# Selective scan: the last-column copies of the scans kept in PSUM, moved from ScalarE to VectorE

## The chip, the cores and the metric

The kernel runs on one core of a Trainium2 chip. Times are microseconds (us) of the device; the figure compared is the median of several executions. The engines are called PE (TensorE; its weight loads are PEld), DVE (VectorE), ACT (ScalarE), POOL (GpSimd) and SP (SyncE, which here only issues DMAs). Each works through a list of its own in order, and an instruction waits at the head of its list until what it needs is done.

## The reference

The program is four network layers on a tensor of 8 images, 64 channels, 64 x 64 pixels. The change is in the fourth, whose core is a recurrence over the 4096 pixels of an image, in four directions `k`, for 128 channels with 16 states each:

```python
def step(h, inp):
    u_t, dt_t, B_t, C_t = inp
    h = h * jnp.exp(dt_t[..., None] * A) + dt_t[..., None] * B_t[:, :, None, :] * u_t[..., None]
    return (h, jnp.einsum('bkcn,bkn->bkc', h, C_t))
```

So a state `h` decays by `exp(dt*A)`, takes in `dt*B*u`, and is read out through `C`, summed over the 16 states.

## The kernel before

**Pairs and stages.** The images are worked in four pairs. `tile_kernel` (L1909) starts with the front of pair 0 (layers 0 to 2 and the sources of layer 3). Then `scans(p)` (L1659) runs the recurrence of pair p, and between its steps it draws pieces of other work from a generator: the back of pair p-1 and the front of pair p+1. While the front is in its attention, `self.dense` is 1. In the last pair there is only back work beside the scans.

**Units and steps.** The 4096 pixels are cut into 8 chunks of `TD` = 512 columns. A unit is one image, one direction and one chunk, 64 units for a pair. `at` counts the chunks of a direction: a chunk starts from the last column of the chunk before, which is kept in `self.carries` (one column per scan of a unit, 16), and the last chunk (`at == NTD - 1`) leaves none. A unit has 8 steps of two states each, and a step has two scans (`j` = 0 and 1), one for each half of the channels: 64 channels by 2 states fill the 128 partitions.

**One step** (`step`, L1756):

- ACT computes `exp(dt*A)` into a PSUM bank `dad` (L1776). The banks come from a ring of three (tag `da`); once the back work of the last pair runs out of its planned share, from that ring and another of three in turn.
- DVE runs the scan over the 512 columns (L1779). Its result goes to SBUF (`hd`), or in place into the PSUM bank (`dad`). How many of the two scans stay in PSUM is `own`: 0 or 1 in turn, and 1, 1, 1, 2 in dense stretches and for the last pair.
- If a next chunk follows, ACT copies the last column of the result to `carries` (L1787).
- The product with C (L1790, L1793) is made by POOL for scans in SBUF and by DVE for scans in PSUM, into `vd`.

Two steps ahead, POOL makes `vd = B * (dt*u)` (L1754, `products`); two or three steps behind, PE sums the products over states (L1805, `sums`). SP fetches rows of B and C for each step into rings of four tiles (L1746, `fetch`), so a fetch waits until the tile four steps back was read. Once per unit `inputs` (L1711) and `spread` (L1731) prepare `dt` and `dt*u` of the next unit: PE matmuls, ACT, one DVE product (L1735), and two DMAs that spread it over partitions (`du`, L1739), issued by SP behind the fetches.

**What orders the work.** Each engine's list is not in the order of the program text. The framework plans it when the program is built, by modelled times; only pairs given to `behind` (L444) are pinned. It also sets all waits. In the trace, DVE's product of a scan in PSUM usually stands one scan later than in the text, behind the first scan of the next step.

Of the kernel before, what the change touches and what calls it, by code (L numbers as in the profile page):

```python
# [24 lines left out]
TD = 512  # L25
NTD = L // TD
# [1133 lines left out]
class _Direct:  # L1160
# [595 lines left out]
    def step(self, i, st):  # L1756

        nc, w, net = self.nc, self.w, self.net
        wk, ps = self.sw, self.ps
        u = self.units[i // 8]  # L1760
        k, c, at, CC, v = u["k"], u["c"], u["at"], st["C"], st["v"]


        n0 = 2 * (i % 8)
        own = 1 + (i % 4 == 3) if u["image"] >= B - 2 or self.dense else i % 2
        rev = k >= 2

        def along(t):
            return t[:, ::-1] if rev else t

        h = wk.tile([P, 2 - i % 2, TD], F32, name="hd", tag=f"h{i % 2}", bufs=2)
        hs = []
        for j in range(2):
            n = n0 + j
            da = self.bank("dad", (P, TD), "da")
            nc.scalar.activation(da, u["du"][:, j, 0], AF.Exp, scale=net.As[:, k, n : n + 1])  # L1776
            first = 0.0 if at == 0 else self.carries[:, n : n + 1]
            to = da if j >= 2 - own else h[:, j]
            nc.vector.tensor_tensor_scan(along(to), along(da), along(v[:, j]), first, ALU.mult, ALU.add)  # L1779
            hs.append(to)  # L1780
            if at < NTD - 1 and (own or j):
                ends = h[:, :, 0] if rev else h[:, :, TD - 1]
                cs = self.carries[:, n0 : n0 + 2]
                if own:
                    ends = to[:, 0:1] if rev else to[:, TD - 1 : TD]
                    cs = self.carries[:, n : n + 1]
                nc.scalar.activation(cs, ends, AF.Copy)  # L1787

        if own == 0:
            st["w"] = nc.gpsimd.tensor_tensor(v, h, self.twice(CC), ALU.mult)  # L1790
        for j in range(2 if own else 0):
            engine = nc.vector if j >= 2 - own else nc.gpsimd
            m = engine.tensor_tensor(v[:, j], hs[j], CC, ALU.mult)  # L1793
            st.setdefault("w", m)

    def sums(self, i, st, after=None):

        nc, w, net = self.nc, self.w, self.net
        wk, ps = self.sw, self.ps
        u = self.units[i // 8]  # L1800
        k, c = u["k"], u["c"]
        if i % 8 == 0:
            u["y"] = ps.tile([P, TD], F32, name="yd", tag="y", bufs=1)
        for j in range(2):
            m = nc.tensor.matmul(  # L1805
                u["y"][self.HALF[j]], lhsT=w["fold"], rhs=st["v"][:, j], start=(i % 8 == 0), stop=(i % 8 == 7)
            )
            if after is not None and j == 0:
                net.behind(m, after)
# [147 lines left out]
```

## Time and profile before

| what | value |
|---|---|
| median of 3 runs (lowest to highest) | 12742.49 us (12727.7 to 12745.85) |
| profiled execution, its own time | 12767.64 us |
| span of that execution | 12765.8 us |
| busy share PE, DVE, POOL, ACT | 77%, 68%, 59%, 55% |
| scans in PSUM, DVE product each (L1793) | 1824 |
| last-column copies by ACT from PSUM (L1787, `carry<-dad`) | 1594, 168 ns each |
| last-column copies by ACT from SBUF (L1787, `carry<-hd`) | 1559, 200 ns each on average |

The busy share of an engine is an average over stages with different limits. The scans begin at about 1848 us; before that the front of pair 0 runs alone. From then on three times an attention stretch (1867 to 2802, 5006 to 5848, 7977 to 8804 us) is followed by the rest of that front and a back (to 10450 us), and the last pair's scans end at about 12650 us. In the waits, "X <- Y: 232.0, 154, 7.7" says that X found its engine idle 232.0 us in all, in 154 cases, 7.7 us at most, until Y was done. In a timeline a bracket gives the idle time before the instruction and what ended it.

### The profile page before, as it was taken

To read this page: it belongs to the slowest core of one execution; us is meant where nothing else is said; L and a number is where in the kernel's file an instruction comes from. 1 tells how busy PE (TensorE), PEld (TensorE's weight loads), DVE (VectorE), ACT (ScalarE), POOL (GpSimd) and SP (SyncE) were. 2 spreads that over 40 slices of the span, in tenths; PEclk is the share of its full clock that TensorE was granted. 3 is DMA by queue.
4 is the path that set the end of the run, shared out by engine and by line. 5 is a ranking of instruction groups with operands and counts; after the bars stand their busy time and mean duration, and the time that the engine had idled before them with its cause. 6 is when DMAs were issued, how large, how long until landed. Compare 5 with 4: busy or idle time off the path is not lost. (4 is left out here: it accounts for less than half of the span.)

```text
span 12765.8 us, 142485 instructions
## 1 busy us (share of the span) xinstructions
PE 9843.7 (77%) x46358; PEld 3333.1 (26%) x46358; DVE 8687.9 (68%) x10259; ACT 7009.2 (55%) x15693; POOL 7550.7 (59%) x3844
## 2 busy tenths in 40 slices
PE   9888879987887667997888756997888855555556
PEld 2255222223342112222443211222433211111111
DVE  0122256777786776668776679467777679998878
ACT  5533247765663655665665555665566365455444
POOL 0000026677776683667776676467777567777874
PEclk9966779997888778998888877998888967777667
DMA  0000024544443462444443454344444356556554
GB/s 19 1 1 1 6 98 145 150 146 133 133 128 111 145 189 81 138 140 145 125 131 113 128 176 144 93 140 142 126 134 129 100 174 183 170 165 186 171 172 123
DMA packets 779703, 1575.84 MB, mean 123 GB/s; under 512 B 89280, under 2 KB 89408, under 8 KB 778176
## 3 DMA queue, kind: packets, MB, share of 16 engines
q1 hardware_dynamic: 754752, 1510.30, 39.4%
q10 hardware_dynamic: 24192, 56.32, 1.2%
q8 instruction: 367, 6.01, 0.2%
q14 instruction: 392, 3.21, 0.1%
HBM read 1197.16 MB, written 100.66 MB: 102 GB/s over the span
## 5 line engine op out<-in xcount | busy, mean ns | idle before, releaser
L1754 POOL TENSOR_TENSOR vd<-B,du 128x1024 f32<-128x1024 f32 x2048 | 4821.4, 2371 | 3295.1 <-DMA B<-rows 2016.1
L1805 PE MATMUL yd<-vd,pack 128*64 128x512 f32 x8192 | 2946.2, 738 | 933.7 <-POOL vd L1793 595.3
L1776 ACT ACTIVATE dad<-du,As 128x512 f32<-128x512 f32 x4096 | 2733.8, 682 | 1122.5 <-DVE vd L1793 458.5
L1779 DVE TENSOR_TENSOR_SCAN hd<-dad,carry,vd 128x512 f32<-128x512 f32 x1992 | 2497.0, 1267 | 480.0 <-ACT dad L1776 324.4
L1793 POOL TENSOR_TENSOR vd<-hd,C 128x512 f32<-128x512 f32 x1290 | 1659.8, 1290 | 1046.7 <-DVE hd L1779 1030.0
L1779 DVE TENSOR_TENSOR_SCAN dad<-dad,carry,vd 128x512 f32<-128x512 f32 x1592 | 2004.8, 1273 | 166.6 <-ACT dad L1776 164.4
L1790 POOL TENSOR_TENSOR vd<-hd,C 128x1024 f32<-128x1024 f32 x491 | 1158.1, 2359 | 735.5 <-DVE hd L1779 406.6
L1307 ACT ACTIVATE e<-s 128x512 f32<-128x512 f32 x2048 | 1200.2, 591 | 628.3 <-PE s L1301 626.5
L1301 PE MATMUL s<-X 64*128 64x512 f32 x4096 | 1435.8, 646 | 79.6 <-ACT e L1307 58.8
L1805 PEld LDWEIGHTS yd<-vd,pack 128*64 128x64 f32 x8192 | 667.0, 160 | 2815.0 <-issue 1214.6
L1793 DVE TENSOR_TENSOR vd<-dad,C 128x512 f32<-128x512 f32 x1824 | 1207.5, 673 | 239.6 <-ACT carry L1787 232.0
L1293 PE MATMUL po<-e,VT 128*64 128x512 f32 x4096 | 1207.8, 623 | 16.9 <-ACT e L1307 10.2
L1459 PEld LDWEIGHTS w_av<-vals,wide 64*64 64x64 f32 x16384 | 678.1, 173 | 209.7 <-ACT wide L1449 106.3
L1459 PE MATMUL w_av<-vals,wide 64*64 64x9 f32 x16384 | 705.6, 224 | 34.8 <-ACT wide L1449 34.6
L1787 ACT ACTIVATE carry<-hd 128x1 f32<-128x1 f32 (+1 forms) x1559 | 307.6, 200 | 697.1 <-DVE hd L1779 681.0
L1301 PEld LDWEIGHTS s<-X 64*128 64x128 f32 x4096 | 393.4, 186 | 1107.5 <-issue 832.6
L1787 ACT ACTIVATE carry<-dad 128x1 f32<-128x1 f32 x1594 | 268.1, 168 | 698.3 <-DVE dad L1779 688.9
L1717 PE MATMUL pdd<-xs,xdt 128*128 128x512 f32 x512 | 375.7, 824 | 334.6 <-issue 103.1
L1444 DVE TENSOR_TENSOR wide<-w_s,bias 128x512 f32<-128x512 f32 x512 | 327.7, 680 | 254.5 <-PE w_s L1431 246.5
L1449 ACT ACTIVATE wide<-wide 128x512 f32<-128x512 f32 x512 | 309.5, 626 | 318.7 <-DVE wide L1444 194.3
L1239 PE MATMUL pv<-n_sq,pack 128*128 128x512 f32 x576 | 364.5, 718 | 144.0 <-ACT n_sq L1237 130.0
L1316 DVE COPY att<-po 128x512 f32<-128x512 f32 x32 | 21.7, 679 | 643.3 <-PE po L1293 643.3
(246 smaller groups left out, 11137.5 us busy)
## 6 DMA issues: line engine op xcount, KB each, us to landing
B<-rows SPq DMA_DIRECT2D x2048, 256.0 KB, 3.6
C<-rows SPq DMA_DIRECT2D x2048, 256.0 KB, 3.5
du<-du SPq DMA_DIRECT2D x512, 512.0 KB, 5.9
xs<-xt SPq DMA_DIRECT2D x128, 256.0 KB, 3.6
xs<-xc SPq DMA_DIRECT2D x128, 256.0 KB, 3.8
xc<-xcv ACTq DMA_DIRECT2D x64, 256.0 KB, 2.1
zs<-z ACTq DMA_DIRECT2D x64, 256.0 KB, 3.8
xt<-XT ACTq DMA_DIRECT2D x32, 512.0 KB, 4.6
```

The source lines that it names most:

```text
L1293: nc.tensor.matmul(po[half[im]], lhsT=VT[:, t, half[im]], rhs=es[im], start=(t == 0), stop=(t == 31))
L1301: nc.tensor.matmul(ss[im], lhsT=at(half[im], t), rhs=X[half[im], jc * CH : (jc + 1) * CH], start=True, stop=True)
L1307: nc.scalar.activation(e, ss[im], AF.Exp, scale=C**-0.5, accum_out=parts[:, im, t, jc : jc + 1])
L1459: nc.tensor.matmul(self.av[half[im], x % 4 + j, h, :], lhsT=es[h // 4][half[im], j, h % 4, :], rhs=V[half[im], x + j, h, :], start=True, s ...
L1717: nc.tensor.matmul(pd, lhsT=net.xdt[:, k, :], rhs=x, start=True, stop=True)
L1754: self.nc.gpsimd.tensor_tensor(v, self.twice(st["B"]), self.units[i // 8]["du"][:, :, 1], ALU.mult)
L1776: nc.scalar.activation(da, u["du"][:, j, 0], AF.Exp, scale=net.As[:, k, n : n + 1])
L1779: nc.vector.tensor_tensor_scan(along(to), along(da), along(v[:, j]), first, ALU.mult, ALU.add)
L1787: nc.scalar.activation(cs, ends, AF.Copy)
L1790: st["w"] = nc.gpsimd.tensor_tensor(v, h, self.twice(CC), ALU.mult)
L1793: m = engine.tensor_tensor(v[:, j], hs[j], CC, ALU.mult)
L1805: m = nc.tensor.matmul(u["y"][self.HALF[j]], lhsT=w["fold"], rhs=st["v"][:, j], start=(i % 8 == 0), stop=(i % 8 == 7))
```

## The change

For scans that stay in PSUM the copy of the last column is taken from ACT and given to DVE, in the program text right behind the DVE product with C. Scans in SBUF keep their copy on ACT: with `own == 0` one copy of two columns after the second scan, else one copy behind the scan that went to SBUF. The condition on the ACT copy changes accordingly.

```diff
@@ -1778,7 +1778,7 @@
             to = da if j >= 2 - own else h[:, j]
             nc.vector.tensor_tensor_scan(along(to), along(da), along(v[:, j]), first, ALU.mult, ALU.add)
             hs.append(to)
-            if at < NTD - 1 and (own or j):
+            if at < NTD - 1 and (j if own == 0 else to is not da):
                 ends = h[:, :, 0] if rev else h[:, :, TD - 1]
                 cs = self.carries[:, n0 : n0 + 2]
                 if own:
@@ -1792,6 +1792,9 @@
             engine = nc.vector if j >= 2 - own else nc.gpsimd
             m = engine.tensor_tensor(v[:, j], hs[j], CC, ALU.mult)
             st.setdefault("w", m)
+            if at < NTD - 1 and j >= 2 - own:
+                end = hs[j][:, 0:1] if rev else hs[j][:, TD - 1 : TD]
+                nc.vector.tensor_copy(self.carries[:, n0 + j : n0 + j + 1], end)
```

## The prediction

> **What bounds the kernel now.** I read the page's first part, then busy time by stretches, because the shares of the whole hide the stages.
>
> ```profile
> span 12765.8 us, 142485 instructions
> PE 9843.7 (77%) x46358; PEld 3333.1 (26%) x46358; DVE 8687.9 (68%) x10259; ACT 7009.2 (55%) x15693; POOL 7550.7 (59%) x3844
> ```
>
> No engine is full. In the stretches the columns are length, then PE, PEld, DVE, ACT and POOL busy:
>
> ```profile
> 1867.00:2802.00 935.00, 900.22 (x2995) 243.49 (x2994) 662.85 (x701) 653.50 (x1877) 653.10 (x350) 0.98 0.50 148
> 2802.00:5006.00 2204.00, 1625.94 (x8918) 607.24 (x8916) 1691.64 (x2011) 1216.12 (x2316) 1559.30 (x759) 0.79 0.45 138
> ...
> 10450.00:11650.00 1200.00, 674.95 (x1450) 149.21 (x1450) 1084.73 (x1156) 623.17 (x1348) 936.87 (x497) 0.73 0.58 175
> 11650.00:12450.00 800.00, 419.81 (x889) 93.06 (x890) 648.52 (x687) 357.09 (x857) 640.01 (x347) 0.69 0.56 174
> ```
>
> So there are four regimes. A, attention (three times, 2604 us): PE 96% busy. B, the rest of fronts and backs (three times, 5979 us): nobody over 80%, DVE and PE lead, each list held up by the others. C1 (1200 us): DVE 90%. C2 (800 us): 81% DVE, 80% POOL, and a pattern that repeats every 32.5 us. C3, the last 200 us of scans: DVE 93%.
>
> Next, the copies and the waits around them, over the whole trace:
>
> ```profile
> L1787 ACT ACTIVATE carry<-dad 128x1 f32<-128x1 f32 x1594 | 268.1, 168 | 698.3 <-DVE dad L1779 688.9 <-issue 5.9
> ```
>
> ```profile
> ACT carry L1787 <- DVE dad L1779: 688.9, 1091, 4.5
> ACT dad L1776 <- DVE vd L1793: 458.5, 508, 9.5
> DVE vd L1793 <- ACT carry L1787: 232.0, 154, 7.7
> ```
>
> The reader is to see two waits that the change touches: ACT stands in front of the copies until the scan is done, and DVE's product stands until ACT has made the copy, though the two only read the same bank. Asked by regime, the 232 us are 8 in A, 51 in B, 38 in C1, 133 in C2.
>
> [...] The trace has small DVE instructions from PSUM at its start, and I go by these:
>
> ```profile
> 14.43 0.16 DVE L363 TENSOR_TENSOR bq<-pbq,pack 128x1 f32<-128x1 f32 x1 [1.45 <-PE pbq L362]
> 14.50 0.15 DVE L365 TENSOR_TENSOR bk<-pbq,pack 128x1 f32<-128x1 f32 x1
> 14.57 0.14 DVE L366 TENSOR_TENSOR bv<-pbq,pack 64x1 f32<-64x1 f32 x1
> ```
>
> They last 0.15 us but follow each other at 0.07: the tail of one lies over the next. Price of a copy in a busy list: 0.07 us. Ends: 0.04 (the closest spacing of small memsets, at 11026.86 and 11026.90) and 0.15 (no overlap). Below nothing it can't be.
>
> **The change, part by part.**
>
> *A.* 538 copies move. On DVE, 58 to 71% busy here, 538 x 0.07 = 38 us vanish in idle time; if PE were not full they would count. PE itself waited 21 us for ACT copies (16.4 at L1301, 4.6 at L1293, its rows in the three stretches); 538 of the 865 copies here are from PSUM, so 13 us belong to them, of which I credit half, since PE's next wait is often close: -7.
>
> *B.* 492 copies cost 34 us of DVE; 51 us of DVE's waits go. What DVE gains or loses here I count with its busy share, 0.77: (34 - 51) x 0.77 = -13. ACT: I followed its timeline behind each copy from PSUM. Of 248 us waited there, 197 are followed by an idle gap at least as long before the list runs on, because the next instruction waits for the same DVE, or for PE; they only change their name. 51 us are not swallowed. ACT is 55% busy, so I credit a quarter: -13. B: about -26, less 1 for the bank below: -25.
>
> *C1.* 299 copies x 0.07 = 21, on DVE at 90%: +19. The waits, 38 us in 17 cases of up to 5.8: with three banks DVE can use at most a product, a scan and a product (0.59 + 1.18 + 0.59 = 2.36, by the distances in the timeline) before it needs the next exponential from the same held-up ACT. Each wait cut at 2.36, they sum to 25. Net -6.
>
> *C2.* Here the largest part of the wait sits, 5.5 us in each of 24 units, and I credit nothing. One period:
>
> ```profile
> 12057.32 3.71 POOL L1793 TENSOR_TENSOR vd<-hd,C 128x512 f32<-128x512 f32 x3
> ...
> 12058.61 0.51 SPq L1746 DMA_DIRECT2D C<-rows  x1
> ...
> 12059.88 1.20 SPq L1739 DMA_DIRECT2D du<-du  x2
> ...
> 12065.03 1.30 ACT L1776 ACTIVATE dad<-du,As 128x512 f32<-128x512 f32 x2 [7.12 <-DMA du<-du]
> 12066.27 0.15 ACT L1787 ACTIVATE carry<-dad 128x1 f32<-128x1 f32 x1
> ...
> 12066.45 0.69 DVE L1793 TENSOR_TENSOR vd<-dad,C 128x512 f32<-128x512 f32 x1 [5.82 <-ACT carry L1787]
> ...
> 12067.44 4.65 POOL L1754 TENSOR_TENSOR vd<-B,du 128x1024 f32<-128x1024 f32 x2 [6.40 <-DMA du<-du]
> ```
>
> ACT's list has the next unit's exponentials ahead of the old unit's copy, and they wait for `du`. DVE's product waits behind both. But what sets the 32.5 us is a ring without DVE: POOL works from the arrival of `du` without a break (23.4 us) until its product frees a C tile at 12058.57, SP issues that fetch, another, then `du` (1.3), `du` takes 7.5 to reach POOL. After the change DVE finishes the old unit while `du` travels, and is then idle for the next. 213 copies (15 us) fit into that idle time too. Zero. *C3*: 49 copies at 93%: +3.
>
> **Release of banks.** An exponential that reuses a bank now waits for the copy behind the product, 0.07 us later, where it waited for product and ACT copy. Behind it on ACT stand other exponentials and the front's activations, and PE waits for those. In the timelines such an exponential (0.68) is done some 0.4 us before its scan, so this costs about 1 us; at most 508 waits x 0.07 = 36. The later scan that reads `carries` comes 8 steps on and waits for nothing.
>
> **Sum.** -7 - 25 - 6 + 0 + 3 = -35 us against the profiled execution's 12767.6 us (span and 1.8 us around it), 12733. That execution is 0.2% above the median of the runs; scaled by 12742.5 / 12767.6, 12708 us.
>
> **Rivals.**
>
> 1. *The waits only change their name* (no change, about 12740). For it: four fifths of ACT's waits in B are swallowed by the next gap, and C2's ring. Then copies and gains cancel: 12733 to 12750.
>
> 2. *The copies lengthen DVE's list where it leads* (slower). Place: B and C, 1053 copies. Price 0.07 us each, 74 us: 12816; at 0.15, 158 us: 12900. It decides when what is recovered from B and C1 falls below the copies' price, that is when DVE, freed from ACT's copy, mostly meets an exponential that isn't ready. For it: C1 and C3 at 90% and more, and that DVE has most of the busy time in B together with PE. Against: 89 us of DVE's own waits in B and C1 go.
>
> 3. *C2 opens as well* (faster). If the new plan of the lists frees the C tile a product earlier on POOL (2.36 us in 24 units, 57 us), or if `du` is asked for earlier: 12708 - 57, and with the cut in C1 removed about 12630. Against it: POOL has no idle time in that ring but for `du`.
>
> That the change doesn't do what it says, a plan that puts the copy ahead of the product, would cost the same 0.07 us.
>
> **How the numbers follow.** A measurement of this kernel can tell about 0.2%, 25 us, from no change: 12717 to 12768. Chances: my sum 0.38 (faster by over 0.2% in 0.30 of it, within in 0.08), rival 1 0.20 (within 0.16, slower 0.04), rival 2 0.30 (slower 0.28, within 0.02), rival 3 0.12 (faster). So faster 0.42, same 0.26, slower 0.32. The range, 12620 to 12815, leaves out the far part of rival 2 (copies over 0.07 us) and of rival 3; my sum's own range is 12670 to 12740.
>
> **What would show it.** L1787 with copies from `hd` alone, 1559; a DVE copy group of about 1594 at 0.13 to 0.16 us; no DVE wait for an ACT copy at L1793; in C2 the period still 32.5 us, with DVE idle in front of a scan, until `du`; C1 shorter by a few us. Wrong would be: a C2 period that moved (the ring was misread, or the plan changed), lists in another order, or DVE's waits for L1776 grown by over 60 us in B.

## The result and the profile after

The changed kernel takes 12824.16 us (median of 6 runs, 12805.62 to 12847.64), the kernel before in the same job 12750.92 us (6 runs, 12727.7 to 12769.78). The ratio is 1.0057, with a 95% interval of 1.0043 to 1.0071: slower by 0.6%, where 0.3% faster was forecast, and 9 us outside the forecast's range. The profiled execution took 12823.53 us.

First the page's first part, of the changed kernel:

```profile
span 12821.7 us, 143131 instructions
PE 9859.6 (77%) x46358; PEld 3345.1 (26%) x46358; DVE 8797.0 (69%) x11853; ACT 6798.8 (53%) x14093; POOL 7545.5 (59%) x3844
```

DVE is busy for 109 us more, ACT for 210 us less; the span is 56 us longer than that of the profile before. Busy time says nothing here on where it went.

The groups of copies (line, engine, tile, shapes, count, busy time and mean ns, then idle time in front):

```profile
L1787 ACT ACTIVATE carry<-hd 128x1 f32<-128x1 f32 (+1 forms) x1559 | 306.9, 199 | 841.2 <-DVE hd L1779 826.6 <-issue 8.4 <-ACT z L1639 0.4
L1797 DVE COPY carry<-dad 128x1 f32<-128x1 f32 x1594 | 231.3, 145 | 0.0
```

And the waits around them (the last line is of the kernel before):

```profile
ACT dad L1776 <- DVE carry L1797: 826.8, 473, 9.2
ACT carry L1787 <- DVE hd L1779: 826.6, 898, 5.1
...
ACT dad L1776 <- DVE vd L1793: 115.8, 66, 8.2
DVE vd L1793 <- DMA C<-rows: 82.2, 52, 6.1
...
ACT carry L1787 <- DVE hd L1779: 681.0, 989, 4.6
```

The change did what it says. ACT keeps the 1559 copies from `hd`, DVE has 1594, and DVE's 232 us of waiting for an ACT copy are gone. The 689 us that ACT stood in front of its PSUM copies are gone too, but nearly all of them come back at other places: ACT's exponentials now wait 826.8 us for DVE's copies and 115.8 us for its products, where they waited 458.5 us for the products, and the wait for `hd` scans in front of the other copies rose from 681.0 to 826.6 us. Together these waits were 1828 us and are 1769 us.

The price of a copy can be read in DVE's timeline (start, duration, instruction):

```profile
12114.71 0.67 DVE L1793 TENSOR_TENSOR vd<-dad,C 128x512 f32<-128x512 f32 x1
12115.30 0.14 DVE L1797 COPY carry<-dad 128x1 f32<-128x1 f32 x1
12115.36 0.68 DVE L1793 TENSOR_TENSOR vd<-dad,C 128x512 f32<-128x512 f32 x1
12115.96 0.14 DVE L1797 COPY carry<-dad 128x1 f32<-128x1 f32 x1
12116.02 1.27 DVE L1779 TENSOR_TENSOR_SCAN hd<-dad,carry,vd 128x512 f32<-128x512 f32 x1
```

A copy lasts 0.145 us, but the next instruction starts 0.06 us after the copy's start (0.065 us is the median over the 1364 copies whose successor did not wait). That is the forecast's 0.07 us.

What nothing in the forecast stood for is the order of the lists. The planner made new ones: without the copies, DVE has the same 10259 instructions in both kernels, but at 4033 places of its list another kind of instruction stands. A count in the lists shows the part that turned out to matter: the scan steps that stand beside the window attention of a front, from its first to its last weighing matmul (`w_av`, L1459), and in the stages behind it. These are the way up to the first write of `taps`, the taps stage (filters of nine taps) until the last such write, and the filter stage until the last `xacc`.

| order | front | window attention | up to the taps | taps | filter stage |
|---|---|---|---|---|---|
| before | 1 | 133 | 23 | 50.5 | 37 |
| before | 2 and 3, each | 125 | 23.5 | 42 | 31 |
| after | 1 | 129 | 24.5 | 53 | 37 |
| after | 2 and 3, each | 133 | 22 | 36.5 | 30 |

The rows of a front have the same sum, so both orders have done the same work at both ends. Next comes busy time by stretches of the kernel before, in the window attention, the taps stage and the filter stage of front 2. The columns are length, then PE, PEld, DVE, ACT and POOL busy with counts, the clock granted to PE as a share of full speed, DMA share and GB/s. These bounds, like those of the attention stretches given ahead of the forecast, lie some 11 us behind the instructions that they are named for on the trace's scale; the lengths are right. The taps stage of these rows runs from its first to its last matmul and so holds some six steps fewer than the table's.

```profile
6066.22:6783.31 717.09, 635.91 (x6446) 315.50 (x6446) 541.03 (x699) 428.03 (x835) 519.12 (x253) 0.84 0.42 126
6918.20:7182.86 264.66, 227.66 (x586) 77.80 (x585) 160.56 (x187) 89.33 (x177) 142.46 (x70) 0.93 0.33 99
7182.86:7429.16 246.30, 143.13 (x260) 35.89 (x258) 192.65 (x251) 165.97 (x259) 141.68 (x69) 0.65 0.47 147
```

and of the changed kernel:

```profile
6035.77:6796.08 760.31, 670.36 (x6396) 329.65 (x6392) 567.66 (x774) 429.99 (x795) 549.72 (x268) 0.81 0.43 125
6930.19:7189.52 259.33, 215.16 (x555) 75.71 (x554) 142.18 (x178) 73.09 (x136) 113.33 (x56) 0.91 0.27 80
7189.52:7433.23 243.71, 138.31 (x254) 34.02 (x252) 190.39 (x262) 160.56 (x239) 138.16 (x67) 0.65 0.47 146
```

POOL's count is about two per scan step. Beside the window attention 15 more stand, and the stretch is 43 us longer; in the taps stage 14 fewer, and it is 5 us shorter. Front 3 shows the same: 717.64 to 761.60 us, and 265.64 to 262.38. Front 1 does not fit the count: it lost four steps and is only 2 us shorter. All other stretches of the profile together are some 20 us shorter than before.

### The profile page after: what moved, and what is told of

Read it like the earlier page. It is cut to its first block, busy times and chain, and to the rows that moved or that the text cites. A ratio compares the mean times of both kernels' runs of the same rounds, so it can differ in the third digit from the quotient of the medians.

```text
span 12821.7 us, 143131 instructions
## 1 busy us (share of the span) xinstructions
PE 9859.6 (77%) x46358; PEld 3345.1 (26%) x46358; DVE 8797.0 (69%) x11853; ACT 6798.8 (53%) x14093; POOL 7545.5 (59%) x3844
## 5 line engine op out<-in xcount | busy, mean ns | idle before, releaser
L1776 ACT ACTIVATE dad<-du,As 128x512 f32<-128x512 f32 x4096 | 2730.2, 680 | 1547.0 <-DVE carry L1797 826.8
L1787 ACT ACTIVATE carry<-hd 128x1 f32<-128x1 f32 (+1 forms) x1559 | 306.9, 199 | 841.2 <-DVE hd L1779 826.6
L1459 PEld LDWEIGHTS w_av<-vals,wide 64*64 64x64 f32 x16384 | 690.7, 176 | 224.7 <-ACT wide L1449 109.2
L1459 PE MATMUL w_av<-vals,wide 64*64 64x9 f32 x16384 | 719.4, 226 | 37.1 <-ACT wide L1449 37.0
L1293 PEld LDWEIGHTS po<-e,VT 128*64 128x64 f32 x4096 | 227.1, 135 | 869.5 <-issue 570.2
```

The costliest lines, as they stand in the source:

```text
L1293: nc.tensor.matmul(po[half[im]], lhsT=VT[:, t, half[im]], rhs=es[im], start=(t == 0), stop=(t == 31))
L1459: nc.tensor.matmul(self.av[half[im], x % 4 + j, h, :], lhsT=es[h // 4][half[im], j, h % 4, :], rhs=V[half[im], x + j, h, :], start=True, s ...
```

## The experiments

Two theories stood at the start. *Copies*: what DVE pays for them is more than the relief brings (rival 2 of the forecast). *Order*: the copies and the relief are about even, and the new order of the lists costs. To part them, the order was pinned.

**Four kernels: copies and order apart.** `_pin` ties each instruction of an engine's list to the one ahead of it by an ordering edge without a wait, from a stored order; a copy by DVE that the stored order doesn't have stands right behind its product. The traces bear this out: without the copies, the lists of DVE, ACT and POOL are, kind by kind, those of the kernel whose order was stored.

```diff
             d.scans(p, d.chain(*works), cost)
+    _pin(tc, net)
...
+def _pin(tc, net):
...
+        prev = None
+        for k in order:
+            for i in [ins[k]] + behind.get(ins[k].name, []):
+                if prev is not None:
+                    tc.add_manual_dep(
+                        i,
+                        prev.name,
+                        mybir.DependencyInfo(mybir.DependencyClass.NoSync, mybir.DependencyReason.DATA),
+                        reason="order on one engine",
+                    )
+                prev = i
```

The change in the old order:

> The copies are made by VectorE as in the change, each right behind its product, but every engine's list is pinned to the order that it has in the kernel before. Theory 1, the new plan of the lists made the change slower: here the sum of the prediction holds, about 12715 us where before is 12751, ratio 0.997. Theory 2, the copies on DVE's list are the cost whatever the order: about as slow as the change, 12800 to 12840, ratio 1.004 to 1.007.

The kernel before, copies on ACT, in the order of the changed kernel (shown against the changed kernel). ACT's copies from PSUM have no place in that order and are left to the planner:

```diff
-            if at < NTD - 1 and (j if own == 0 else to is not da):
+            if at < NTD - 1 and (own or j):
...
-            if at < NTD - 1 and j >= 2 - own:
-                end = hs[j][:, 0:1] if rev else hs[j][:, TD - 1 : TD]
-                nc.vector.tensor_copy(self.carries[:, n0 + j : n0 + j + 1], end)
```

> The other half: the copies stay on ScalarE, but every engine's list is pinned to the order that it has in the changed kernel (the ScalarE copies from PSUM are placed freely between). Theory 1: the new order alone is slow, 12800 us or more, ratio 1.005 or more. Theory 2: the order is worth nothing, ratio 0.998 to 1.002, about 12750.

The old order with the PSUM copies left out, shown against the kernel before. The columns are zeroed once, so the scans of later chunks start from zeros or from what another unit left there:

```diff
-            if at < NTD - 1 and (own or j):
+            if at < NTD - 1 and (j if own == 0 else to is not da):
```

> Lists pinned to the order of before, and the last-column copies of the scans in PSUM are left out, on ScalarE and on VectorE: later chunks of those scans start from zero. What is left is the gain of taking the copies from ACT. By the prediction's credits (7 in A, 52 in B, 25 in C1, nothing in C2) 84 us faster, about 12667, ratio 0.993. Under theory 2 the waits only change their name: ratio 0.997 to 1.000. The distance to the kernel with VectorE's copies in the old order is the price of these copies there: 48 us by the prediction, 74 and more by its second rival.

The old order with both, ACT's copy and DVE's of the same column, against the kernel before:

```diff
             st.setdefault("w", m)
+            if at < NTD - 1 and j >= 2 - own:
+                end = hs[j][:, 0:1] if rev else hs[j][:, TD - 1 : TD]
+                cp = nc.vector.tensor_copy(self.carries[:, n0 + j : n0 + j + 1], end)
+                net.added[cp.ins.name] = m.ins.name
```

> Lists pinned to the order of before, ScalarE's copies stay, and VectorE makes the same copies once more right behind its products. So nothing is relieved and the 1594 copies are only added. By the prediction's shares (0 in A, 26 in B, 19 in C1, 0 in C2, 3 in C3) 48 us slower, 12799, ratio 1.004. Second rival: 74 to 112 us, ratio 1.006 to 1.009. If they hide in idle time: ratio 1.000 to 1.002.

Measured, as ratios to the kernel before in the same job (12743.74 us, 19 runs):

| PSUM copies | old order | new order |
|---|---|---|
| ACT | 1 | 1.0112 [1.0097, 1.0127], 12879.58 us |
| DVE | 0.9997 [0.9988, 1.0006], 12740.4 us | 1.0057 [1.0043, 1.0071], the result |
| left out | 0.9966 [0.9954, 0.9979], 12707.46 us | |
| both | 1.0043 [1.003, 1.0056], 12793.05 us | |

In the old order the change makes no difference that can be told. The new order costs 0.60% with DVE's copies and 1.12% with ACT's; how much of the 1.12% comes from the places that the planner gave ACT's copies is not known. So *copies* falls as the cause, and *order* stands. The last two rows size the terms: taking ACT's copies away without a substitute is worth 0.34% (43 us); the DVE copies cost 0.31% (40 us, left out against DVE) to 0.43% (55 us, both against before). The medians themselves give a little less, 36 us, 33 us and 49 us.

**Four kernels: moving the scans against the front.** If the number of steps beside the window attention is what counts, moving steps alone should show it. In the stored lists, all instructions of the scan stream were shifted against those of the front, by whole steps, in the course of the window attention, and shifted back in the taps and filter stages; each stream kept its own order. The edit is a table of positions, told here in words:

```diff
-shift of the scans at the end of the window attention of fronts 1, 2, 3, in steps: 0, 0, 0 (old order)
+8 earlier in fronts 2 and 3 (old order)
+8 later in fronts 2 and 3 (new order)
+8 later in fronts 1, 2 and 3 (old order)
+16 later in fronts 1, 2 and 3 (old order)
```

> VectorE copies in the order of the kernel before, with one thing moved: in pairs 2 and 3 the scan stream is laid 8 steps earlier against the front in the course of the window attention (133 steps beside it, as in the changed kernel, where the old order has 125) and falls back by 8 in the taps and filter stages. Theory 'steps beside the window attention': a step costs 5.7 us there (717 us for 126, 760 for 133) and gives back about 0.9 us in the stages that it leaves (265 to 259 us for 6): 12740 + 2 x 8 x 4.8 = about 12817. Rival 'local order' (which instruction stands ahead of which inside a step): 12740 within 15 us. Rival 'lower clock or copies': no change against 12740.

> The changed kernel in its own order, with the reverse move: in pairs 2 and 3 the scan stream is held back by 8 steps in the course of the window attention (125 beside it in place of 133) and catches up in the taps and filter stages. Theory 'steps beside the window attention': 12824 - 2 x 8 x 4.8 = about 12747. Rival 'local order': it stays at 12824 within 20 us.

> VectorE copies in the order of the kernel before, the scan stream held back by 8 steps in the window attention of all three fronts beside scans (118, 118 and 125 steps, from 125, 125 and 133), caught up in the taps and filter stages. Theory 'steps beside the window attention': these stages run at 7.3 us a step and scans alone at about 5, so that they have room for some 16 steps more each: 12740 - 3 x 8 x 4.8 = about 12625; if the room is not there, 12740. Rival 'local order': 12740 within 15 us, or slower because any move from the planned order costs.

> The same with 16 steps held back (109.5, 109.5 and 117 steps). Theory 'steps beside the window attention': 12740 - 3 x 16 x 4.8 = about 12510 if the taps and filter stages hold 16 more; where they are full after 8, 12625 to 12700. Rival 'local order': not below 12725.

Measured: 13194.12 us (1.0356 [1.034, 1.0371]), 13297.38 (1.043 [1.0414, 1.0447]), 13408.01 (1.0519 [1.0504, 1.0535]) and 13552.64 (1.0629 [1.0613, 1.0645]). No theory expected that. In the second of them the window attention of front 2 took 907 us for 125.5 steps, 7.2 us a step, where the planner's orders give 5.7, and even the stage behind it, shifted by a constant 8 steps, took 165 us for 27.5 steps where the old order takes 135 for 27. So something other than the number of steps was changed by the shift, most likely the fine order inside the steps, and these runs don't tell what the number does. Two things moved along, by the traces. In the window attention of front 2 the granted clock was 0.73 to 0.76 in the four kernels, where the old order has 0.83 and the new one 0.81 (over the whole execution 0.795 to 0.805, where the old order with DVE's copies has 0.816 and the new one 0.811). And ACT had more table loads (`ACT_TABLE_LOAD`, 1.28 us each): 391 to 421 in place of 343 in the new order and 349 in the old. In the first of the four the exponentials of the scans had 115 loads for 87, and the activations at L1526 of the kernel before 88 for 64. All added loads come to 61 to 92 us on ACT, a seventh of the loss at most; the rest was not taken apart. What the runs do show is that an order that is wrong in detail can cost several times what the change cost.

**Four kernels: other plans.** The pace at which the front is drawn into the scans in the program text is set by costs (`yield`). Other costs make the planner produce other numbers of steps, each in an order of its own.

```diff
             last = (x, es)
-            yield 7
+            yield 6.8
         weigh(*last)
         following = ahead()
-        yield 5
+        yield 4.9
...
-        yield 4
+        yield 3.9
         return following
```

> The changed kernel, with the pace costs of the window attention set to 6.8, 4.9 and 3.9 in place of 7, 5 and 4, and a plan of its own from that. Counted in the lists, 128, 128 and 128 scan steps stand beside the window attention of the three fronts, where the changed kernel has 129, 133 and 133 (and the kernel before 133, 125 and 125). Theory 'steps beside the window attention' (5.7 us a step there, 0.9 given back elsewhere, so 4.8 net): 12824 - 11 x 4.8 = about 12771. Rival 'every new plan is a draw': nothing follows from the count; anything from 12720 to 12900, with the loss at other places than the window attention.

The same with 6.6, 4.7 and 3.8:

> The changed kernel with pace costs of 6.6, 4.7 and 3.8: 129.5, 128.5 and 128.5 steps. Theory 'steps': 12824 - 8.5 x 4.8 = about 12783, and the window attention of fronts 2 and 3 at 5.7 us a step, about 735 us each in place of 760. Rival 'draw': no relation between the count and the stretch.

On the kernel before, 6.8, 4.9 and 3.9, and then 6.2, 4.4 and 3.5:

> The kernel before (ScalarE copies) with pace costs of 6.8, 4.9 and 3.9: 127, 125.5 and 125.5 steps in place of 133, 125 and 125. Theory 'steps': 12744 - 5 x 4.8 = about 12720; the first window attention shorter by some 33 us, the taps stage behind it longer. Rival 'draw': 12744 give or take 60 us.

> The kernel before with pace costs of 6.2, 4.4 and 3.5: 132.5, 123.5 and 123.5 steps. Theory 'steps': 12744 - 3.5 x 4.8 = about 12727. Rival 'draw': 12744 give or take 60 us, with differences at other places than the window attention.

Measured: 12808.17 us (1.0051 [1.0038, 1.0064]), 12839.93 (1.0065 [1.0051, 1.008]), 12789.13 (1.0033 [1.0021, 1.0044]) and 12752.77 (1.0005 [0.9997, 1.0013]). The first part of the theory held: in the changed kernel with 6.8, the window attention of fronts 2 and 3 took 739 and 738 us for 128.5 steps, 5.7 us a step, and over the three fronts the stretch gave back 54 us. In all 36 such stretches of the twelve kernels with planned orders (the two below among them) a step takes between 5.5 and 5.8 us. The second part failed: of the 54 us, 38 were lost elsewhere. The steps did not go back to the taps stage (30 there, as in the changed kernel: 30.5), but that is not the whole of it: the three stretches between attention and window attention took 24 us more for the same number of steps (129 for 129.5). So the total does not follow one count, and the order inside a stretch counts as well; that the loss lies where the steps come from and go to was the theory left for the last two runs. The third kernel was slower by 0.33% where 0.2% faster was expected; its profile, taken in its fastest execution (12747 us), shows no stretch that explains the median, and this stays open.

**Two kernels: the suspected stretches swapped.** Since both orders agree on what is done at the start of the window attention and at the end of the filter stage, the stretch between can be exchanged whole, each part in an order that a plan has made.

```diff
 order = the order of the kernel before, DVE copies behind their products
+        fronts 2 and 3, from the first w_av matmul to the last xacc: as in the changed kernel
```

> VectorE copies in the order of the kernel before, except for two stretches of the lists, from the first weighing matmul of the window attention to the end of the filter stage of fronts 2 and 3, which stand as in the changed kernel (133, 22, 36.5 and 30 scan steps in the four stages in place of 125, 23.5, 42 and 31; both orders have done the same steps at both ends). Theory 'steps moved out of the taps and filter stages to beside the window attention': the loss is all in these stretches, +43 - 9 us each: 12740 + 70 = about 12810. Rival 'the loss is spread over the new order': under 12770.

```diff
 order = the order of the changed kernel
+        fronts 2 and 3, from the first w_av matmul to the last xacc: as in the kernel before
```

> The reverse: the changed kernel in its own order, except for the same two stretches, which stand as in the kernel before. Theory 'steps moved': 12824 - 70 = about 12754. Rival 'the loss is spread': above 12790.

Measured, against 12735.8 us for the kernel before (19 runs): 12789.51 us (1.0043 [1.003, 1.0056]) and 12744.14 us (1.0003 [0.9994, 1.0013]). Putting the two stretches into the old order costs 0.46% (1.0043 against 0.9997, 59 us), taking them out of the new one recovers 0.54% (1.0057 against 1.0003, 69 us). That is most of the 0.60%, or 76 us. The first of these comparisons is between two pinned kernels, so the pinning is not the cause either. The stretches of the first kernel, the old order with the new stretches, are the window attention and taps stage of front 2, then the window attention of front 3:

```profile
6035.73:6790.99 755.26, 666.88 (x6475) 326.80 (x6474) 569.65 (x777) 434.76 (x802) 550.70 (x269) 0.82 0.42 126
6925.12:7184.43 259.31, 215.17 (x554) 75.57 (x553) 142.13 (x178) 73.49 (x136) 113.02 (x56) 0.91 0.27 80
...
9007.36:9764.12 756.76, 666.25 (x6411) 327.51 (x6410) 569.56 (x775) 434.19 (x801) 549.44 (x268) 0.82 0.42 126
```

and of the second, the new order with the old stretches:

```profile
6030.02:6741.82 711.80, 631.89 (x6386) 312.62 (x6384) 536.14 (x751) 418.78 (x775) 517.58 (x252) 0.83 0.42 126
6876.83:7142.11 265.28, 228.64 (x586) 78.18 (x585) 161.62 (x201) 87.26 (x163) 142.49 (x70) 0.92 0.33 98
...
8977.74:9704.67 726.93, 649.08 (x6443) 323.01 (x6444) 540.46 (x752) 421.75 (x779) 517.55 (x252) 0.81 0.41 124
```

The lengths go with the order of the stretch, whatever stands around it: in front 2, 43 us more in the window attention and 6 us less in the taps stage, and in front 3, 30 us more. A lower clock is not the cause, since in front 3 the longer stretch had the higher clock, 0.82 against 0.81. Between these two fronts the longer stretch did have the lower clock: as many steps took 711.80 us at 0.83 in front 2 and 726.93 at 0.81 in front 3.

What fits is that eight more steps stand beside the window attention. That stretch takes 5.5 to 5.8 us a step in every plan, whereas the taps stage is hardly shorter with six steps fewer (259.31 for 265.28 us), so there was room beside it. But the swap exchanged the counts and the fine order together. That the count alone costs the time is argued from the constant pace, with front 1 against it, and not shown. What sets the pace was not isolated either; PE, the busiest engine, stands at 88 to 89% there. No version was found that beats the kernel before.

## Why the prediction was wrong

**The step that failed** is the sum itself: it took the lists of before, with copies put in, as the lists of after. Its part by part held terms for copies, waits and banks and none for a new order; "the new plan of the lists" came up only in rival 3, as a chance of gain, and "lists in another order" only among the things that would make it wrong. The runs showed that the new order cost 76 us, most of it in two fronts between the start of the window attention and the end of the filter stage, where the planner had moved eight steps out of stages with room to beside the window attention. All three rivals missed it too; rival 2 forecast about the right time, 12816, but by luck, for a reason that the runs refute.

**With the lists kept**, the sum can be tested, since the pinned kernel is what it describes. It gave -35 us; measured is 0.9997 [0.9988, 1.0006], -4 us with an interval of -15 to +8.

- *The copies' price*: 0.07 us a copy and 49 us in all after weighting with DVE's busy share (26 in B, 19 and 3 in C, 1 for the banks). Measured 40 to 55 us. Right.
- *The relief*: 84 us credited (7 in A, 52 in B, 25 in C1). Measured 43 us with the copies left out. This term was twice too large, and badly placed. Stretch by stretch, the kernel without the copies is shorter than the kernel before by 19, 14 and 8 us in the three attention stretches, which the forecast credited with 7, by 21 us in B in place of 52, and by nothing in the 595 us from 10443 us on (from 10380 us without the copies), which fall into C1:

| stretch | before | left out, old order | DVE copies, old order |
|---|---|---|---|
| attention 1, 2, 3 | 936, 842, 827 | 917, 828, 819 | 922, 830, 823 |
| window attention 1, 2, 3 | 744, 717, 718 | 740, 710, 715 | 733, 717, 720 |
| C, first 595 us | 595 | 595 | 595 |
| C, next stretch | 1388 | 1388 | 1384 |

These are single profiled executions, and 10 us between them mean little: the first window attention, 733 us here in the old order with DVE's copies, took 744 in the first kernel of the swap, where nothing ahead of its end differs; and the execution of before was itself 24 us above its median. The gain in attention recurs, though: in the old order with both copies, where ACT is not relieved, the three stretches took 943, 848 and 844 us. For A there is a likely reason: PE, 96% busy there, waited for ACT copies in its weight loads as well, and only the 21 us of the matmuls were counted. In the kernel before, over the whole trace:

```profile
PEld s L1301 <- ACT carry L1787: 36.4, 43, 2.3
...
PEld po L1293 <- ACT carry L1787: 17.3, 16, 3.4
```

Both are gone from the kernel without the copies; that they are the whole of the gain was not tested. C1 speaks against the cut waits: DVE is at 90% there and was relieved of waits, and nothing came of it.

- *C2 at nothing*: right. The first exponentials of the units follow each other at a median of 32.7 us before and after. The wait that went was replaced, as the timeline of the changed kernel shows (SPq is SP's queue):

```profile
12119.57 1.20 SPq L1739 DMA_DIRECT2D du<-du  x2
...
12125.16 1.30 ACT L1776 ACTIVATE dad<-du,As 128x512 f32<-128x512 f32 x2 [5.28 <-DMA du<-du]
...
12127.62 6.96 POOL L1754 TENSOR_TENSOR vd<-B,du 128x1024 f32<-128x1024 f32 x3 [6.58 <-DMA du<-du]
...
12142.20 0.69 DVE L1793 TENSOR_TENSOR vd<-dad,C 128x512 f32<-128x512 f32 x1 [3.84 <-DMA C<-rows]
```

POOL still stands until `du` arrives, and DVE's product now waits for a row of C. The product's wait for ACT's copy, 133 us in C2 before and 232 us in all, is gone as forecast. Why the product stood until the copy was done, though both only read the bank, was not shown. That the wait went was worth little, and in the period shown the list behind it was held by something else.

- *Rival 1*, waits that only change their name: this is what the pinned kernel shows, within 0.1%. Of the forecast's cases it came nearest to the mechanism.
- *What would show it*: DVE's waits for L1776 in B grew from 200 to 225 us, under the 60 us that would have spoken for rival 2. "Lists in another order" is what came.

## What to carry to other kernels

Where a planner orders the lists, any edit that adds or moves an instruction is two changes, the edit and a new plan, and the second can be the larger: forecast it with a spread of its own (here the planner's own kernels lay up to 0.65% above the kernel before), and measure the edit with the order pinned. Look for stages in which a piece of background work is free and others in which it costs its full time (here, in front 2 of the swap, the taps stage was 6 us shorter with six steps fewer, the window attention 43 us longer with eight more), and count in the new lists how many pieces went from one to the other; here that count pointed to the right stretches, but did not forecast the total. A wait that is removed counts only if the list behind it can run; the 232 us of DVE's waits and the 689 us in front of ACT's copies came to 43 us.

## What the runs showed of the hardware

In the changed kernel a 128x1 copy from PSUM by DVE took 0.145 us by its record (mean of 1594), but the next instruction of a busy list started 0.065 us after it (median). The same copy by ACT took 0.168 us in the kernel before. And a shift of one stream against the other by whole steps, each stream in its own order, took a step from 5.7 to 7.2 us beside the window attention of front 2 in one kernel. In the four kernels with a shift the granted clock there was 0.73 to 0.76 in place of 0.81 to 0.83, and ACT had 391 to 421 table loads in place of 343 to 349. Such a shift cost 3.6% to 6.3%, where the copies that the change touched were worth 0.3% to 0.4%.
